# 32 instead of 40 early expert tiles, cut from all but the third row's last 128 tokens, and a new written order for four engines

## The chip, the cores and the metric

One core of a Trainium2 chip runs the whole program. The metric is the device time of one execution in microseconds (us); the kernel before took 429.48 us as the median of three runs (428.34, 429.48 and 429.67). The engines are called PE (matmul), DVE (vector), ACT (scalar), POOL (GpSimd) and SP (the queue that issues most loads). Each engine works through its instructions in order; an instruction that waits holds all behind it.

## The reference

A batch of 4 rows of 512 tokens of 256 features passes a gated linear recurrence with complex state and then a mixture of experts with 32 experts, of which each token takes 6.

```python
x = x + attn(layernorm(x))        # xh = x@W_in; gates; h[t] = a[t]*h[t-1] + xc[t]; h@W_out
xf = layernorm(x).reshape(-1, 256)            # 2048 tokens
scores = sigmoid(xf @ gate_w.T)               # 32 experts in 8 groups
# the 4 groups with the largest maxima stay; the 6 best experts of these are taken
w = chosen_scores / sum(chosen_scores) * 2.5
g, u = xf @ w11[e].T, xf @ w33[e].T           # per expert, 128 wide
y = sum_e  w[t, e] * (silu(g) * u) @ w22[e].T
shared = (silu(xf @ sw1.T) * (xf @ sw3.T)) @ sw2.T
x = x + y + shared
```

All of it is fp32.

## The kernel before

**First part, row by row.** For each row b of 512 tokens the kernel makes the gates (g), the angles (a), the rotated inputs (f) and the scans of the recurrence (s), then the output matmuls with the layer norm and the scores (t), the routing (r) and the shared expert (h). Work of row b+1 is woven into the work of row b. In the lists below a letter with a number names such a piece: r2 is the routing of row 2 (the third row), t3 the attention output of row 3.

**Routing.** `route` (line 522) finds each token's six experts on DVE. Its last products are the weights and `pos` (line 575), the rows of a table `xg` in device memory where the token is to stand, ordered by expert. POOL then issues 24 scatters a row, 4 groups of 128 tokens by 6 choices (`xg<-row,pos`, line 579), 128 rows of 320 numbers each. In rows 0 and 1 a small memset follows each scatter (line 589). A running sum of tokens by expert, `count` (lines 592 and 593), goes from row to row.

**Second part, tiles of 128 tokens of one expert.** The kernel has 112 usual tiles, worked as 56 pairs. `read` (l, line 822) loads a pair's rows from `xg` on the SP queue, four pairs ahead, into four buffers. `spread` (x) transposes them on PE (line 839), ACT copies them (841), DVE picks weights and places (844 to 851). `weights` (k) copies the two experts' up-weights on DVE (859). `up` (u) is 8 matmuls of the pair (871), a silu on ACT (873) and a product on DVE (875). `down` (d) is the second matmul (885), a scaling on ACT (889) into one of six buffers (b_u, b_p, b_th, b_kk, b_s, b_c, by pair number modulo 6), and two scatters on POOL into `zz` (891). At the end the six parts of each token are read back from `zz` (977), added, transposed and written out.

**Early and late tiles.** Which expert a tile belongs to depends on the counts. `tables` (line 651, the pieces ne and nl) makes a table of tiles out of `count`. The early one is made after row 2's routing, from full groups of 128 tokens alone, and its first EARLY tiles may be read before row 3 is routed: their reads wait only for the scatters listed up to then (`puts[:first]`). All other tiles come from the late table and their reads wait for every scatter into `xg`.

**What sets the order.** For PE, DVE, ACT, POOL and SP the kernel holds a written list, `ORDERS`, in which an item such as `r3:24` takes the next 24 instructions of piece r3. `in_order` chains each engine's instructions in that order up to the end of the usual tiles. POOL's lists count two instructions for one scatter (three in rows 0 and 1), PE's list counts matmuls. Every fourth d and k and l item of PE, DVE and SP also loads a few registers.

Of the kernel before, what the change touches and what calls it, by code (L numbers as in the profile page):

```python
# [19 lines left out]
P = 128  # L20
# [29 lines left out]
EARLY = 40  # L50
assert EARLY <= (TOPK * (B - 1) * T - E * (P - 1) + P - 1) // P
# [8 lines left out]
        "g0:24 g1:4 t0 g1:2 t0:4 g1 t0:2 g1 t0 g1:16 g2:8 t0:23 t1 t0 t1:4 h0:2 t1 t0:8 h0 r0 g2 h0 g2:3 t1 g2:4 t1 "  # L60
        "r0:5 g2:8 h0:4 g3:4 t1:3 g3 t1:4 g3:3 t1:9 h0:8 t1:8 h1:3 t2 t1:8 t2:5 r1 h1 g3:4 r1 g3:8 r1:4 t2:2 g3:4 h1:2 "
        "t2:16 h1:9 t2 h1 t2:12 h2:4 t2:3 t3 h2:4 r2:4 t3:2 r2:2 h2:3 t3:4 ne h2:5 t3:7 ne t3:5 d0 ne t3:13 h3:3 t3:3 "
        "h3 t3:5 h3:4 r3:6 h3:5 nl h3 x0:4 h3:2 x1:4 u0:8 x2:4 u1:8 d0 x3:4 d0 u2:8 d1 x4:4 u3:8 d1 d2:2 u4:2 x5:4 u4:6 "
        "d3:2 x6 u5 x6:3 u5 d4 nl u5:6 d4 u6:5 d4 u6:3 nl x7:4 x8:4 d5:2 d6 u7:8 x9 d6 x9:3 x10:4 u8:8 u9:2 x11:2 u9:2 "
        "x11 u9:4 x11 d7:2 x12 u10:2 x12:2 u10:3 x12 u10:3 x13 d8:3 d9 u11:5 d9 u11 x13:2 u11:2 x13 u12 d10:2 u12:5 "
        "x14:3 u12:2 x14 d11 u13:3 x15 u13 d11 u13:2 d12 u13:2 u14:3 d12 x15:3 d12 u14:3 x16:2 u14:2 x16:2 x17:2 u15:2 "
        "d13 x17:2 u15:6 u16 d13 d14 x18 u16:5 d14 x18:3 u16:2 u17:2 x19 d15:2 d16 u17:2 x19:3 u17:4 u18:8 x20:2 d16 "
        "x20:2 d16 d17:2 u19 x21 u19 x21:3 u19:6 d18 u20 x22:3 u20:7 x22 x23 d18 d19 x23 u21:5 d19 x23 d20 x23 u21:3 "
        "u22:2 d20:2 u22:6 u23 x24:4 u23 d21:2 u23:6 d22 x25:4 d22 x26:2 u24 x26:2 u24:7 d23:2 u25:7 d24 u25 x27:4 x28 "
        "u26:3 x28:3 u26:5 u27:2 d24:2 d25 x29:2 d25 x29:2 u27:2 x30:2 u27:4 u28 d26 u28:3 d26 x30 u28:4 x30 d27:2 "  # L70
        "u29:2 d28 u29:2 x31 u29:4 x31:3 x32:3 u30:2 x32 x33 d28:2 u30:6 u31 x33 d29 x33:2 d29 u31:6 x34 u31 u32:6 "
        "x34:2 d30:2 u32:2 x34 x35:4 d31 u33 d31 u33:7 d32:2 u34:4 x36 u34 x36 u34:3 d32 x36:2 u35:2 d33 u35:2 x37 "
        "u35:4 x37 d33 x37:2 u36:3 d34 u36 d34 x38 d35:2 u36:4 u37 x38:2 d36 x38 x39 u37 x39:2 u37 x39 u37:5 d36:2 "
        "u38:2 x40:2 u38:6 x40:2 u39:3 d37 u39 x41:2 d37 u39:3 x41:2 u39 u40:3 d38 x42 d38 u40:5 d39 u41:2 x42:3 d39 "
        "u41:3 x43 u41:3 d40:3 x43:3 x44:3 u42 x44 u42:7 u43:2 d41 u43:4 x45 d41 u43:2 u44:2 x45:2 u44:2 x45 x46 u44:2 "
        "d42:2 u44:2 x46:3 x47 u45:2 x47 u45:3 d43 x47 d43 u45 d44 x47 u45 x48 u45 u46 d44:2 u46:6 x48 u46 x48:2 x49 "
        "d45 u47 x49 u47 x49 u47:5 x49 u47 d45 u48:2 x50:4 u48:6 d46:2 d47:2 d48 u49:4 x51 u49:4 d48 x51:3 d48 x52 u50 "
        "x52 u50:7 x52:2 d49:2 x53:3 u51:5 x53 u51:3 d50:2 u52:3 x54 u52:5 x54:3 x55:2 d51:2 x55 u53:8 x55 d52:3 u54:8 "
        "d53:2 u55:8 d54:2 d55:2",
    ET.DVE:  # L80
        "c cc:3 c:5 cc:11 c:3 cc:3 g0 cc g0:2 c g0:2 c g0:17 cc g1 a0 g1 cc a0:2 g1 a0:2 c a0 g1 a0:2 f0 g1 a0 g1:5 a0 "
        "g1:4 a0 g1:8 a0:2 f0 a0:2 f0 a0:2 f0:2 s0 a0:3 s0:8 a1 g2 a1 g2:2 a1 g2:2 a1 g2 a1:4 t0 g2 t0:2 a1:2 t0:2 g2 "
        "t0:17 f1 a1 f1:2 a1:5 f1 a1 f1 s1 r0:26 a1 r0 a1:2 r0 s1 r0:6 s1:3 h0 r0 s1:3 a2 s1 a2:3 r0 a2:4 f2 h0 g3 a2 "
        "t1 g3:5 t1:2 g3 t1:2 g3 t1:17 a2 f2 a2:5 f2 a2:2 f2:2 s2 a2:2 r1 a2 r1 s2 r1:4 s2:2 r1:28 s2:5 a3:8 h1 t2 a3:2 "
        "t2:2 a3 t2:10 h1 t2:9 f3 a3 f3 a3:4 f3:2 r1 a3 r1 f3 s3 a3:3 h2 s3:2 r2:23 s3 r2 h2 r2:12 s3:2 ne s3:3 ne:15 "
        "t3 ne t3:2 k0 x0 t3:3 ne t3:16 h3 r3 k0 r3:21 h3 r3:2 k0 k1 r3:12 k1 x0:3 nl x1:3 u0 nl:2 k2 nl k2 k3 x1 k3 u1 "
        "x2:3 k4 nl:2 k4:2 u2 x2 x3:2 nl:2 x3:2 x4:3 k5:2 x4 nl u3 k6:2 nl:6 x5 nl:3 x5 u4 x5:2 x6:2 nl:3 u5 q0 k7:2 x6 "
        "u6 x6 x7 k8 x7 nl:2 k8:2 k9:2 nl x7:2 x8:4 x9:2 u7 q1 k10:2 u8 k11 x9 k11 k12 x9 x10:4 x11:2 k12:2 u9 u10 q2 "
        "x11 k13 x11 k13 x12:4 k14 u11 x13:2 u12 k14 x13:2 x14 k15:2 k16:3 u13 x14:3 x15:2 u14 x15:2 x16:2 k17:2 k18:2 "
        "x16:2 x17:2 u15 u16 x17:2 x18:3 u17 k19:2 k20 x18 x19:2 k20 u18 x19:2 k20 k21:2 k22:2 x20 u19 x20 k23 x20:2 "  # L90
        "x21:3 k23 u20 x21 x22:2 k24:2 x22:2 u21 x23:2 k24 k25:2 u22 k26 x23:2 x24:4 u23 k26 k27 x25:4 k27 x26:2 u24 "
        "x26:2 q3 u25 x27 k28:2 x27 k28 k29 x27 u26 x27 x28:4 x29:3 u27 k29 u28 k30:2 k31 x29 x30:2 k31 k32 x30:2 u29 "
        "k32 x31:4 u30 x32:2 k32 k33:2 u31 k34:2 x32 u32 x32 k35 x33:4 x34 k35 u33 k36 x34:3 u34 x35:2 k36:2 x35:2 "
        "k37:2 u35 x36:4 k38:2 k39 x37:4 x38:4 u36 x39:2 u37 k39 k40:3 u38 k41:2 x39:2 k42 x40:2 u39 x40:2 x41 k42 x41 "
        "k43:2 x41:2 x42 u40 k44:2 x42:3 x43:2 k44 x43:2 x44 u41 k45 x44:3 x45:2 u42 k45 x45 u43 u44 k46 x45 k46 x46:2 "
        "k47 u45 k47 x46:2 x47 k48 x47 k48 u46 x47:2 x48:2 k48 k49 u47 k49 x48:2 k50:2 x49 k51:2 u48 x49 k52 x49:2 "
        "x50:2 u49 x50:2 x51:2 k52:2 x51:2 x52:2 k53 u50 x52:2 x53:4 u51 k53 x54 k54:2 k55 x54 k55 u52 u53 x54 u54 x54 "
        "x55:4 u55",
    ET.Activation:
        "cc b0:2 g0:9 a0:2 g0:3 a0:8 g1:2 a0 g1:2 a0 g1:2 a0:2 b1:2 g1:4 a1:2 g1:2 a1:8 t0:4 p0:2 a1 t0:2 a1:2 t0 g2:4 "  # L100
        "a1 g2:4 h0 g2 a2:2 g2:3 h0 a2:3 b2:2 a2:4 h0:2 t1:4 a2:2 t1:2 a2 p1:2 a2:2 t1 g3:8 h1 g3 b3 a3:2 g3:3 a3:2 h1 "
        "a3:2 b3 a3:5 t2:4 h1:2 t2:2 a3:3 h2 p2 t2 p2 h2:3 t3:2 p3 t3:2 p3 t3:2 h3 t3 h3:2 x0 x1 u0 x2 h3 u1 x3 u2 d0:2 "
        "x4 u3 d1:2 x5 u4 d2:2 x6 u5 d3:2 d4:2 u6 x7 x8 u7 x9 d5 u8 x10 d5 d6:2 u9 x11 d7 u10 d7 d8:2 x12 d9 x13 u11 d9 "
        "d10:2 u12 x14 d11 u13 x15 d11 d12:2 u14 x16 u15 x17 x18 u16 d13:2 d14:2 u17 d15:2 x19 x20 d16 u18 d16 d17:2 "
        "u19 x21 u20 d18:2 x22 u21 x23 d19:2 u22 d20:2 x24 d21 u23 d21 d22 x25 d22 x26 u24 u25 x27 x28 d23:2 u26 d24:2 "
        "d25:2 u27 x29 x30 u28 d26:2 d27:2 x31 u29 d28 x32 u30 d28 u31 x33 d29:2 u32 d30 x34 d30 x35 u33 u34 x36 d31:2 "
        "d32:2 u35 d33:2 x37 d34:2 d35:2 u36 x38 u37 x39 u38 x40 d36:2 d37 u39 x41 d37 u40 d38:2 d39 x42 d39 u41 x43 "
        "d40:2 u42 x44 d41:2 u43 x45 d42:2 u44 x46 d43:2 u45 x47 u46 x48 d44:2 u47 d45:2 x49 x50 u48 d46:2 d47:2 u49 "
        "x51 d48:2 x52 u50 d49 u51 d49 x53 d50:2 u52 x54 d51:2 u53 x55 d52:2 u54 d53:2 u55 d54:2 d55:2",
    ET.Pool:  # L110
        "c:10 r0:72 r1:71 r2:48 r3:24 d0:4 d1:2 r3:4 d1:2 d2:4 r3:2 d3:4 d4:4 d5:4 d6:2 r3:8 d6:2 r3:10 d7:4 d8:4 d9:4 "
        "d10:4 d11:4 d12:4 d13:4 d14:4 d15:2 r1 d15:2 d16:4 d17:4 d18:4 d19:4 d20:4 d21:4 d22:4 d23:4 d24:4 d25:4 d26:4 "
        "d27:4 d28:4 d29:4 d30:4 d31:4 d32:4 d33:4 d34:4 d35:4 d36:4 d37:4 d38:4 d39:4 d40:4 d41:4 d42:4 d43:4 d44:4 "
        "d45:4 d46:4 d47:4 d48:4 d49:4 d50:4 d51:4 d52:4 d53:4 d54:4 d55:4",
    ET.SP:
        "c i0 c:7 i1 c:3 w:10 i2 c:3 w c w:54 p0 i3 h0 p1 h1 wl:2 p2 wl h2 l0 wl:5 p3 l0:2 l1:2 l2:2 l3:2 l4:3 l5:2 h3 "
        "l6:2 l7 o0 l7 l8 o0 l8:2 o1 l9:2 l10:2 o1 l11:2 l12:3 l13:2 o2:2 l14:2 o3 l15:2 l16 o3 l16:2 l17:2 l18:2 l19:2 "
        "l20:3 l21:2 l22:2 l23:2 l24:3 l25:2 l26:2 l27:2 l28:3 l29:2 l30:2 l31:2 l32:3 l33:2 l34:2 l35:2 l36:3 l37:2 "
        "l38:2 l39:2 l40:3 l41:2 l42:2 l43:2 l44:3 l45:2 l46:2 l47:2 l48:3 l49:2 l50:2 l51:2 l52:3 l53:2 l54:2 l55:2",
}  # L120


@with_exitstack
def kernel(ctx, tc, x, w_in, w_gx, w_ga, vecs, w_out, gate, w11, w33, w22, sw1, sw3, sw2, out):

# [378 lines left out]

    idle = const.tile([1, 256], mybir.dt.bfloat16, name="idle")
    count = const.tile([P, E], F32, name="count")  # L510
    V.memset(count, 0.0)

    def scores(b, xn2):
        pl = (ps_m if b < B - 1 else ps_x).tile([P, NT, E], F32, tag="m" if b < B - 1 else "x1", name=f"pl_{b}")
# [543 lines left out]
```

## Time and profile before

| what | value |
|---|---|
| median of three runs | 429.48 us |
| the profiled execution, whole | 428.31 us |
| its span, first to last instruction | 426.4 us |
| mean granted clock of PE | 0.916 |
| PE busy | 346.3 us, 81% of the span |
| DVE busy | 303.1 us, 71% |
| ACT busy | 231.8 us, 54% |
| POOL busy | 236.4 us, 55% |
| scatters into xg, 96 | 105.6 us, mean 1.10 |
| scatters into zz, 112 | 115.0 us, mean 1.03 |

The profiled execution took 428.31 us, of which the span is 426.4 us; the other 1.9 us lie before the first and after the last instruction. A timeline row gives the start and the duration in us, the engine, the line, the operation with what it writes and reads, the number of instructions, and in brackets the idle time of the engine before it with what ended that time. Lines are those of the kernel before.

### The profile page before, as it was taken

The numbers are of one execution on the slowest core, as the hardware profiler recorded it, in microseconds if no ns is written. First come the engines' busy times: TensorE is split into PE (matmuls) and PEld (weight loads), VectorE is DVE, ScalarE is ACT, GpSimd is POOL, SyncE is SP. The second block draws the span as 40 slices with busy tenths as digits, with TensorE's granted clock in tenths as the row PEclk, the third lists the DMA queues.
The fourth block names the chain that finished last, engine by engine and source line by source line (L and its number), as shares of the span: only waits on it lengthen the run. The fifth ranks groups of instructions, "written<-read, shape, count | busy, mean of one in ns | idle before, by whom it ended". The sixth has DMA issues, their size and how long they took to land.

```text
span 426.4 us, 7569 instructions
## 1 busy us (share of the span) xinstructions
PE 346.3 (81%) x2074; PEld 281.8 (66%) x2074; DVE 303.1 (71%) x995; ACT 231.8 (54%) x435; POOL 236.4 (55%) x269
## 2 busy tenths in 40 slices
PE   1754787897999888499999999999999999930376
PEld 1332266455646546356999999999999999920276
DVE  5169989999999999517588755776586567412884
ACT  2399957698978871151455545655464555520023
POOL 1000000088879998775777777777777777750000
PEclk9995986999799899978999999999999999995569
DMA  5999871124422375684999966665565655227996
GB/s 154 367 279 302 244 214 49 50 78 157 158 86 100 137 255 206 226 323 154 332 317 358 361 222 203 223 211 170 161 203 177 198 184 190 92 70 309 419 412 240
DMA packets 63868, 91.58 MB, mean 215 GB/s; under 512 B 8517, under 2 KB 53069, under 8 KB 63824
## 3 DMA queue, kind: packets, MB, share of 16 engines
q1 hardware_dynamic: 52000, 56.18, 41.8%
q0 software_dynamic: 9984, 28.33, 17.8%
q10 hardware_dynamic: 1840, 6.55, 3.8%
q8 instruction: 18, 0.29, 0.3%
q14 instruction: 26, 0.21, 0.2%
HBM read 51.19 MB, written 41.94 MB: 218 GB/s over the span
## 4 chain that ended last, share of the span: by engine, by line
PE 42%; DMA 9%; POOL 2%; issue 1%; SPq 0%; ACT 0%; ACTq 0%; POOLq 0%
PE gu L871 22%; PE y L885 11%; PE pxt L839 6%; DMA w_all<-zz 5%; DMA zz<-b_u,place 2%; PE pz L1001 2%; PE pz L1002 2%; POOL zz L891 1%; DMA b_x<-xg 1%; POOL xg L579 1%; DMA xg<-row,pos 1%; SPq L822 0%; ACT o L1004 0%; ACTq L977 0%; PE pbl L711 0%
## 5 line engine op out<-in xcount | busy, mean ns | idle before, releaser
L579 POOL DMA_INDIRECT xg<-row,pos x96 | 105.6, 1100 | 110.0 <-ACT xh L395 83.1
L885 PE MATMUL y<-w_all,b_ga 128*128 x224 | 60.8, 381 | 0.1
L875 DVE TENSOR_TENSOR b_ga<-b_gx,gu 128x256 f32<-128x256 f32 x56 | 23.4, 417 | 37.2 <-ACT b_gx L873 33.2
L873 ACT ACTIVATE b_gx<-gu 128x256 f32<-128x256 f32 x56 | 21.6, 386 | 40.7 <-PE gu L871 36.3
L885 PEld LDWEIGHTS y<-w_all,b_ga 128*128 128x128 f32 x224 | 36.7, 191 | 2.8 <-DVE b_ga L875 0.7
L1001 PE MATMUL pz<-ident,w_all 128*128 128x128 f32 x64 | 14.9, 321 | 27.6 <-DVE w_all L997 17.3
L1001 PEld LDWEIGHTS pz<-ident,w_all 128*128 128x128 f32 x64 | 11.8, 230 | 28.3 <-issue 17.7
L1004 ACT COPY o<-pz 128x256 f32<-128x256 f32 x16 | 5.9, 373 | 39.8 <-DVE w_all L987 30.1
L987 DVE TENSOR_TENSOR w_all<-w_all 128x768 f32<-128x768 f32 x14 | 13.2, 957 | 18.9 <-DMA w_all<-zz 18.9
L891 POOL DMA_INDIRECT zz<-b_u,place x20 | 21.9, 1095 | 6.2 <-issue 1.8
L891 POOL DMA_INDIRECT zz<-b_p,place x20 | 20.2, 1010 | 6.1 <-issue 1.8
L841 ACT COPY b_sphi<-pxt 128x512 f32<-128x512 f32 x28 | 16.4, 585 | 12.0 <-PE gu L871 6.2
L891 POOL DMA_INDIRECT zz<-b_c,place x18 | 18.6, 1032 | 5.6 <-issue 2.1
L849 DVE TENSOR_REDUCE cd<-pick 128x4 f32<-128x128 f32 x56 | 15.8, 281 | 8.3 <-ACT b_c L889 3.1
L841 ACT COPY b_cphi<-pxt 128x512 f32<-128x512 f32 x28 | 16.3, 584 | 9.6 <-PE pxt L839 7.9
L891 POOL DMA_INDIRECT zz<-b_s,place x18 | 18.3, 1017 | 5.5 <-issue 1.8
L891 POOL DMA_INDIRECT zz<-b_th,place x18 | 18.2, 1009 | 5.5 <-issue 2.4
L891 POOL DMA_INDIRECT zz<-b_kk,place x18 | 17.8, 989 | 5.3 <-issue 1.5
L358 PE MATMUL pt<-ident,row 128*128 128x128 f32 x32 | 9.7, 404 | 12.9 <-ACT row L350 7.0
L394 PE MATMUL ph<-xn,win_sb 128*128 128x512 f32 x32 | 18.3, 723 | 1.1 <-ACT xn L359 1.1
L358 PE MATMUL pt<-ident,xnt 128*128 128x128 f32 x32 | 7.4, 358 | 14.2 <-ACT xnt L350 14.2
L647 PE MATMUL sy<-s,sa 128*128 128x256 f32 x64 | 17.3, 416 | 1.1 <-DVE sa L640 1.1
(350 smaller groups left out, 1065.5 us busy)
## 6 DMA issues: line engine op xcount, KB each, us to landing
w_all<-in_w_dram SPq DMA_DIRECT2D x64, 128.0 KB
w_all<-zz SPq DMA_DIRECT2D x7, 768.0 KB
w_all<-zz ACTq DMA_DIRECT2D x7, 768.0 KB
xg<-blank SPq DMA_DIRECT2D x1, 5120.0 KB
b_xh<-xg SPq DMA_DIRECT2D x28, 160.0 KB
b_x<-xg SPq DMA_DIRECT2D x28, 160.0 KB
b_xn<-xg SPq DMA_DIRECT2D x28, 160.0 KB
b_xnt<-xg SPq DMA_DIRECT2D x28, 160.0 KB
```

Source lines behind the costliest of these rows:

```text
L358: PE.transpose(pt[:, j * P : (j + 1) * P], src[j][:, k * P : (k + 1) * P], ident)
L394: PE.matmul(ph, win_sb[:, k, m * P : (m + 1) * P], xn[:, k], start=(k == 0), stop=(k == KC - 1))
L579: i = GP.indirect_dma_start(out=xg[:, :], out_offset=bass.IndirectOffsetOnAxis(ap=pos[:, t, k : k + 1], axis=0), in_=row[:, t], in_offset= ...
L647: PE.matmul(py[:, i], a[:, k, j * P : (j + 1) * P], s2[:, k], start=(k == 0), stop=(k == NSH - 1))
L839: PE.transpose(pt[:, i, k], rows[:, i, k * P : (k + 1) * P], ident)
L841: A.copy(xt, pt)
L871: PE.matmul(gu[:, w, i], w1[:, k, w], xt[:, i, k], start=(k == 0), stop=(k == KC - 1))
L873: A.activation(s, gu[:, 0], AF.Silu)
L875: V.tensor_tensor(a, s, gu[:, 1], ALU.mult)
L885: m = PE.matmul(py[:, i], a[:, i], w2[:, bass.ds(e, 1)].rearrange("p o d -> p (o d)"), start=True, stop=True)
L891: s = GP.indirect_dma_start(out=zz.rearrange("t k d -> (t k) d"), out_offset=bass.IndirectOffsetOnAxis(ap=place[:, i : i + 1], axis=0), in ...
L1001: PE.matmul(pt[:, k], z[:, 0, cut], ident, start=True, stop=False)
```

## The change

EARLY falls from 40 to 32. The early table is now made from a new sum `sure`, which leaves out the last 128 tokens of row 2: two more DVE instructions add it up. The last six scatters of row 2 no longer hold the early reads, so these wait for 66 scatters instead of 72. The lists of PE, DVE, ACT and POOL are new; in SP's list only `h3` and the items `o0`, `o1` (reads of the tokens' own part) move by a few places.

```diff
-EARLY = 40
-assert EARLY <= (TOPK * (B - 1) * T - E * (P - 1) + P - 1) // P
+EARLY = 32
+assert EARLY <= (TOPK * ((B - 1) * T - P) - E * (P - 1) + P - 1) // P
...
     ET.PE:
...
-        "t2:16 h1:9 t2 h1 t2:12 h2:4 t2:3 t3 h2:4 r2:4 t3:2 r2:2 h2:3 t3:4 ne h2:5 t3:7 ne t3:5 d0 ne t3:13 h3:3 t3:3 "
-        "h3 t3:5 h3:4 r3:6 h3:5 nl h3 x0:4 h3:2 x1:4 u0:8 x2:4 u1:8 d0 x3:4 d0 u2:8 d1 x4:4 u3:8 d1 d2:2 u4:2 x5:4 u4:6 "
...
+        "h2:2 t2:4 h2:4 t2:4 r2 h2:2 r2 t3:3 h2 t3:2 h2 r2:4 h2 t3:2 h2:5 t3 ne t3:10 ne t3:5 d0 ne t3:9 h3 t3 h3:2 "
+        "t3:7 h3 r3 h3:4 r3:5 h3 x0:4 h3:5 x1:4 nl h3:2 u0:8 x2:4 u1:8 d0:2 x3:2 u2 x3:2 u2:7 u3:2 x4:4 u3:2 d1 u3 d1 "
...
     ET.DVE:
...
-        "t0:17 f1 a1 f1:2 a1:5 f1 a1 f1 s1 r0:26 a1 r0 a1:2 r0 s1 r0:6 s1:3 h0 r0 s1:3 a2 s1 a2:3 r0 a2:4 f2 h0 g3 a2 "
-        "t1 g3:5 t1:2 g3 t1:2 g3 t1:17 a2 f2 a2:5 f2 a2:2 f2:2 s2 a2:2 r1 a2 r1 s2 r1:4 s2:2 r1:28 s2:5 a3:8 h1 t2 a3:2 "
-        "t2:2 a3 t2:10 h1 t2:9 f3 a3 f3 a3:4 f3:2 r1 a3 r1 f3 s3 a3:3 h2 s3:2 r2:23 s3 r2 h2 r2:12 s3:2 ne s3:3 ne:15 "
-        "t3 ne t3:2 k0 x0 t3:3 ne t3:16 h3 r3 k0 r3:21 h3 r3:2 k0 k1 r3:12 k1 x0:3 nl x1:3 u0 nl:2 k2 nl k2 k3 x1 k3 u1 "
...
+        "a1 f1 a1:5 f1:2 a1:2 f1 s1 r0:14 a1 r0:2 a1:2 r0:2 s1 r0:9 s1 r0:6 h0 r0 s1:4 a2 s1:2 a2 g3 a2:2 g3 a2 g3 a2:2 "
+        "h0 a2 t1 f2 t1:2 r0 g3 t1 a2 g3 t1 g3:2 t1:2 g3 t1:15 a2:3 f2:2 a2:5 f2:2 s2 a2 r0 a2 r1 a2 r1:9 s2 r1:2 s2 "
+        "r1:4 s2 r1:11 s2 r1:7 s2 r1 s2:3 a3:5 t2:3 a3:3 h1 a3 t2:14 h1 t2:5 f3 a3:3 f3 a3 f3 a3:3 f3 a3 f3 h2 s3 a3:3 "
+        "r2 s3 r2:4 s3 r2:5 r1 r2 s3 r2:7 h2 r2:7 s3 r2:10 s3 r2 s3:3 r2 ne:14 t3:3 ne:3 t3:5 r2 t3 k0 t3:4 x0 t3:9 "
+        "r3:6 h3 r3:21 h3 r3:9 ne x0:3 k0:2 x1:4 x2 k1:2 k2:2 k3:2 u0 x2:2 nl:2 k4 x2 nl x3:3 u1 nl:2 x3 x4:3 k4:2 nl "
...
     ET.Activation:
...
-        "a1 g2:4 h0 g2 a2:2 g2:3 h0 a2:3 b2:2 a2:4 h0:2 t1:4 a2:2 t1:2 a2 p1:2 a2:2 t1 g3:8 h1 g3 b3 a3:2 g3:3 a3:2 h1 "
...
-        "x4 u3 d1:2 x5 u4 d2:2 x6 u5 d3:2 d4:2 u6 x7 x8 u7 x9 d5 u8 x10 d5 d6:2 u9 x11 d7 u10 d7 d8:2 x12 d9 x13 u11 d9 "
...
+        "u1 d0:2 x3 u2 x4 d1 u3 x5 d1 u4 d2:2 d3:2 x6 u5 d4:2 x7 x8 u6 d5:2 u7 x9 u8 x10 d6:2 d7:2 x11 u9 u10 x12 d8:2 "
+        "u11 x13 x14 u12 d9:2 d10:2 u13 x15 x16 u14 d11:2 d12:2 x17 u15 u16 d13:2 d14 x18 d14 u17 x19 d15:2 u18 d16:2 "
...
     ET.Pool:
-        "c:10 r0:72 r1:71 r2:48 r3:24 d0:4 d1:2 r3:4 d1:2 d2:4 r3:2 d3:4 d4:4 d5:4 d6:2 r3:8 d6:2 r3:10 d7:4 d8:4 d9:4 "
...
+        "c:10 r0:72 r1:71 r2:48 r3:14 d0:2 r3:6 d0:2 r3:6 d1:4 d2:4 r3:22 d3:4 d4:4 d5:4 d6:4 d7:4 d8:4 d9:4 d10:4 "
...
@@ route
-                if b == B - 1:
+                if b == B - 1 or (b, t) == (B - 2, NT - 1):
                     tc.add_to_no_dep_group("last", i.ins)
...
         more = sm("more", E)
+        if b == B - 2:
+            V.tensor_reduce(more, sel[:, : NT - 1].rearrange("p t e -> p e t"), AX.X, ALU.add)
+            V.tensor_tensor(sure, count, more, ALU.add)
...
@@ after the rows
-    first = len(puts)
-    early, taken = tables(True, None)
+    first = len(puts) - TOPK
+    early, taken = tables(True, None, sure)
...
-    late, _ = tables(False, taken)
+    late, _ = tables(False, taken, count)
```

How the lists move single instructions, engine by engine, is told in the prediction where a step needs it.

## The prediction

> **What bounds the kernel now.** I read the busy slices first, then POOL's timeline, then the timelines of DVE, SP, PE and ACT at the places that POOL's gaps point to, and last the end of the chain of waits.
>
> ```profile
> PE   1754787897999888499999999999999999930376
> DVE  5169989999999999517588755776586567412884
> POOL 1000000088879998775777777777777777750000
> ```
>
> A slice is 10.66 us. PE is full from slice 18 to 33, and DVE from slice 3 to 14. POOL shows only 7 in the pair phase, but a scatter is 0.97 busy and the next starts 0.30 later at the soonest, so 7 is POOL working back to back.
>
> ```profile
> 126.08 1.14 POOL L579 DMA_INDIRECT xg<-row,pos  x1 [2.03 <-issue]
> ...
> 164.49 1.00 POOL L579 DMA_INDIRECT xg<-row,pos  x1 [0.17 <-issue]
> 165.79 0.98 POOL L579 DMA_INDIRECT xg<-row,pos  x1 [0.30 <-issue]
> ...
> 188.04 0.97 POOL L579 DMA_INDIRECT xg<-row,pos  x1 [0.30 <-issue]
> ...
> 195.73 1.09 POOL L579 DMA_INDIRECT xg<-row,pos  x1 [0.30 <-issue]
> 199.58 0.97 POOL L579 DMA_INDIRECT xg<-row,pos  x1 [2.76 <-issue]
> ...
> 376.46 0.97 POOL L891 DMA_INDIRECT zz<-b_u,place  x1 [0.40 <-ACT b_u L889]
> ...
> 380.29 0.97 POOL L891 DMA_INDIRECT zz<-b_p,place  x1 [0.30 <-DMA zz<-b_u,place]
> ```
>
> These are the first and last scatter of row 1, the first, 18th and last of row 2, the first of row 3 and two of the last. Between 126 and 380 POOL stands only once for more than its step: 2.76 before row 3. From there 136 scatters run without a hole, (380.29 - 199.58) / 135 = 1.339 each. Gaps of 0.40 near the end, released by ACT's scaling, say that PE and ACT are just in time there. After the last scatter the read-back starts at 385.01 and the rest ends at 426.4: a fixed tail of 46.1 after the last scatter's start. So the end is: start of row 3's scatters, plus 135 steps, plus the tail.
>
> ```profile
> 125.12 0.18 DVE L575 TENSOR_SCALAR pos<-top 128x32 int32<-128x32 f32 x1
> 125.21 2.33 DVE L501 TENSOR_TENSOR_SCAN g<-ga,y 128x512 f32<-128x512 f32 x2
> ...
> 198.63 0.18 DVE L575 TENSOR_SCALAR pos<-top 128x32 int32<-128x32 f32 x1
> ```
>
> pos of row 1 ends at 125.30 and POOL starts 0.78 later; in row 3 it is 198.81 and 0.77. In rows 1 and 3 pos is what POOL waits for. In row 2 pos stood ready at 163.07, 2.7 before its first scatter, so row 2 follows row 1 without a hole.
>
> **The change, part by part.** I walk each queue in the new order with the durations of before.
>
> Row 0's pos. L452 (0.68) stood at 60.16, in the shadow of DVE's wait that ended at 61.95; it now comes after L482, inside the full stretch: about +0.6. ACT puts four normalisations L350 (1.93 together) ahead of the sigmoid's table load, which makes `grp` 1.1 later (about 77.3 for 76.19). On DVE L497 (0.68) and L640 (0.66) move ahead of L575. Of this 3.0, some 0.7 overlaps the wait for ACT: pos ends about 87.0 instead of 84.61. Row 0's scatters then end near 126.1 instead of 123.8. That binds nothing unless row 1's pos is as early as before.
>
> Row 1's pos. One scan L501 (pitch 1.15) now runs ahead of L575 instead of behind it; of the earlier lateness 0.55 to 1.1 is left, the rest being work that has moved behind pos. So pos ends 1.7 to 2.25 later; I take 1.7, since DVE's work ahead of it, added up, is the surer count. Row 1's scatters start at 127.8, with a gap before them as now.
>
> Row 2. POOL goes on without a hole, so +1.7: its last scatter is at 197.4 and POOL is free for the next at 197.4 + 1.09 + 0.30 = 198.8. Row 2's pos has 2.7 of slack and takes the moved scan (1.15); the two added DVE instructions for `sure` (like L592 and L593, 0.36 + 0.19) go behind it, where DVE has holes (9.97 before L640 at 189.84), so I cost them at nothing.
>
> Row 3's pos. What it removes: two passes of the shared expert ahead of the scores, 0.87 as they run at 188.63 to 190.60 and up to 1.7 as at 183.76; three weight copies L859 (0.43, 0.40, 0.42, of which two stand right in the route at 195.97). What it adds: one L640 (0.68). That makes pos end near 197.6 instead of 198.81, and POOL could take it at 198.4. POOL itself is free at 198.8 (above), so this is late by 0.4 no more: row 3 starts at 198.8 instead of 199.58, **-0.8**. The hole of 2.76 closes to 0.30 (-2.46) and 1.7 of that is eaten by row 1.
>
> A page rule bears on the two passes, and nothing below rests on it. In the rows L638 takes 0.90 a pass at 183.76 and 0.49 after 188, PE having come out of a thin stretch. The Trainium skill, "TensorE: Matmul & The Clock Gate", Part 1, says the slow warm-up is a budget of about 3.4 us of time, not a number of matmuls. By that rule dropping two passes does not drop slow ones, and saves 0.87, not 1.7; the sum is the same by either, as POOL's own end decides.
>
> The early read. It waits for 66 scatters, so for the 18th of row 2: 188.04 + 1.7 = 189.7 instead of 195.73.
>
> ```profile
> 198.54 0.90 SPq L822 DMA_DIRECT2D b_xh<-xg  x2
> ```
>
> The read was issued 2.8 after the last scatter's start, so now at 192.5, 6 us sooner, and the rows are there at 195.4 (2.87 after issue, as at 201.41 now). But PE is then at row 3's routing and the first output passes; the first transpose comes near 196.8 (201.5 now) and the first pair's up matmul at 200.9:
>
> ```profile
> 203.69 0.50 PE L871 MATMUL gu<-b_sphi,b_wph 128*128 128x128 f32 x3
> ```
>
> So PE gains 2.8 on POOL's 0.8 and begins the pairs with more lead.
>
> The later reads. Pair 16 (l16) was early and is now late: it waits for row 3's last scatter. That one moves from POOL slot 38 to slot 30, so to 198.8 + 29 x 1.339 = 237.6, landed 240.2. Before, l16 was issued at 240.08. Nothing is lost. SP's moved items (one load for the shared expert, two reads of the tokens' own part) pass reads of 0.33 to 0.9 us in a queue that waits for slots anyway; POOL's one leftover instruction of row 1 moves from d15 to d12. Both at nothing; if SP's order held a pair's read back, its lead of four pairs (4 x 3.10) is the cover.
>
> The ring of six buffers. Row 3's scatters end sooner, so d3 moves to slots 31 and 32 and d4 and on behind it, and d9's scaling waits for d3's second scatter: 240.3 + 3.4 (as the b_p row below follows 252.57) = 243.7.
>
> ```profile
> 256.01 0.84 ACT L889 ACTIVATE b_p<-y,cd 128x256 f32<-128x256 f32 x2
> ...
> 246.07 0.60 PE L885 MATMUL y<-w_all,b_ga 128*128 x2
> ```
>
> PE's new order has u14, x15 and x16 to run meanwhile; d12's y needs the space that d10's scaling frees (243.7 + four scalings of 0.85 pitch with what lies between: 247.2), and PE gets there about 245.2: it stands about 2.0. At 246.07 before, PE was at the same pair d12; it then has done 2.1 more of other work (five y of 0.22, nine up passes of 0.11). So of its 2.8 lead about 1.0 is left (247.2 - 246.07 against 2.1), and 0.8 is what POOL's earlier start needs. Bounds: -2.8 if PE never stands, +2.6 if it stands one more round of two scatters.
>
> The sum for the profiled execution: 428.31 - 0.8 = 427.5. Its time is 1.17 under the median of 429.48; the same -0.8 on the median gives **428.7**. The steps' bounds: row 1 later by 1.7 to 2.25 adds 0.55; row 1 not late at all takes 1.7 off, till the whole 2.46 is won.
>
> **The rivals.**
> A, the forecast: -0.8, 428.7. For it: the two gaps in the rows and POOL's hole-free run.
> B, row 1 is not late (DVE's holes elsewhere swallow the moved scan, or the row 0 lateness does not reach it), and pos 3 comes sooner still: -2.46, 427.0. Against it: no DVE hole over 0.15 between 63 and 171.
> C, PE and not POOL sets the end: 56 pairs of 3.10 (16 x 0.11 + 4 x 0.22 + transposes) is 173.2, which is just the time from 203.69 to the last y near 376.9; then the whole -2.8 counts, 426.7. For it: the 0.40 gaps released by ACT. Against it: only five of 135 gaps are longer than 0.31.
> D, **slower**: the ring of six. In ACT's new order d9's and d10's scalings stand ahead of u13 and x15, so while ACT waits at 243.7 for d3's landing, silu and copies behind it wait too, DVE's product after them, and PE with that. It decides as soon as PE reaches d12's equivalent later than 246.07 by more than the 0.3 that POOL's gaps allow. Price: one round of two scatters, 2.6, so 429.48 + 2.6 = 432.1. For it: in before PE lost nothing at d13 although d7's scaling waited to 256.01, because PE was behind; a PE that leads meets the wait.
> E, row 1 is late by 3.0 (the pr matmuls of row 0 now queue behind 3.6 us of L394): POOL then ends row 2 at 200.1 and row 3 starts 0.5 later than now, 430.0. For it: POOL has no slack between row 1 and row 2.
>
> **How the numbers follow.** About 0.3% (1.3 us) is what a measurement of this kernel can tell from no change: 428.19 to 430.77 counts as the same. A has 0.38, B 0.20, C 0.14, D 0.19, E 0.09. A lies 0.5 above the lower bound with an own spread of some 1.2, so a third of it is faster (0.13), the rest the same; B and C are faster but for a tenth (0.31); D is slower (0.18), E splits (0.06 the same, 0.03 slower), and of A 0.02 is slower. Faster 0.43, same 0.34, slower 0.23. The likeliest's own range is 427.5 to 429.9; with B, C and D's nearer part 426.0 to 431.8.
>
> **What would show it.** Row 1's first scatter at 127.8, later than 126.08; row 3's at 198.8 with a gap near 0.30 before it; the first early read issued near 192.5; the first up matmul near 200.9; PE standing some 2 us about 245; the steps of 1.339 unbroken. It is wrong if row 1 starts no later (B), if the last scatters wait for ACT by more than 0.3 each (C or D, by their start), or if the mean step after row 3's start differs from 1.339 by 0.01, which alone is 1.35 us.

## The result and the profile after

The changed kernel takes 425.92 us (median of 20 runs, 424.61 to 430.32) against 428.79 for the kernel before in runs beside it (20 runs, 426.88 to 431.87): a ratio of 0.994 with an interval of 0.9922 to 0.9958, about 2.6 us (the two medians differ by 2.87). It is faster, by three times what was forecast. Its profiled execution has a span of 423.7 us against 426.4.

First the same three rows of busy slices, then POOL's timeline of the kernel after: the first scatter of row 1, the first, 18th and last of row 2, the first of row 3, and the late ones.

```profile
PE   1735859996999889399989999999999999930376
DVE  6089989999999998357777376567477656412884
POOL 1000000098898998777777777777776767750000
```

```profile
125.09 1.01 POOL L580 DMA_INDIRECT xg<-row,pos  x1 [0.17 <-issue]
...
164.13 0.97 POOL L580 DMA_INDIRECT xg<-row,pos  x1 [0.31 <-issue]
...
195.03 1.07 POOL L580 DMA_INDIRECT xg<-row,pos  x1 [0.30 <-issue]
...
327.31 0.97 POOL L896 DMA_INDIRECT zz<-b_p,place  x1 [2.12 <-ACT b_p L894]
...
350.07 1.03 POOL L896 DMA_INDIRECT zz<-b_kk,place  x1 [2.18 <-ACT b_kk L894]
...
377.83 0.97 POOL L896 DMA_INDIRECT zz<-b_p,place  x1 [0.31 <-issue]
```

Both holes of before, 2.03 ahead of row 1 and 2.76 ahead of row 3, are closed; row 3 starts at 195.03 instead of 199.58, 4.55 earlier. But the last scatter comes only 2.46 earlier (377.83 for 380.29). Between them stand two new holes of 2.12 and 2.18, released by ACT's scaling of PE's results: POOL waits for PE. PE's row has an 8 in its 21st slice, in the pair phase, where before it was full. The next three are rows of SP's, PE's and ACT's timelines of the kernel after:

```profile
188.48 0.90 SPq L827 DMA_DIRECT2D b_xh<-xg  x2
```

```profile
196.24 1.05 PE L876 MATMUL gu<-b_sphi,b_wph 128*128 128x128 f32 x8
...
215.31 1.10 PE L890 MATMUL y<-w_all,b_ga 128*128 x4 [1.63 <-DVE b_ga L880]
...
243.97 0.44 PE L844 MATMUL pxt<-ident,b_x 128*128 128x128 f32 x2 [1.31 <-DMA b_x<-xg]
244.49 1.99 PE L890 MATMUL y<-w_all,b_ga 128*128 x8
```

```profile
243.97 0.47 ACT L894 ACTIVATE b_s<-y,cd 128x256 f32<-128x256 f32 x1 [1.61 <-DMA zz<-b_s,place]
```

PE's pairs start 7.45 earlier than before (196.24 for 203.69), and PE then stands 3.84 in the pair phase: 1.63 behind DVE, 1.31 at 244, which is put down to the rows of pair 17, the second of the late ones, and 0.90 (at 261) behind the ring of six buffers. Before it stood for nothing there. The ACT row is the ring itself: the scaling of pair 10 waits until pair 4's scatter has landed, which is at the moment when pair 17's rows come.

In the table, "u" is the first up matmul of pair 0, "y" the start of the last down matmul, and the last column the start of the last scatter; "stands" adds PE's gaps over 0.12 in the pair phase. All are times of one profiled execution, in us. Those of e1, e2 and e4 lie -2.0, +1.8 and +2.2 from the medians of their kernels, so that landmarks of two rows compare only to about that.

| kernel | row 3's first scatter | u | PE stands | y | last scatter |
|---|---|---|---|---|---|
| before | 199.58 | 203.69 | 0 | 376.49 | 380.29 |
| after | 195.03 | 196.24 | 3.84 | 374.03 | 377.83 |
| e1_head60 | 196.24 | 200.49 | 0.17 | 373.59 | 377.39 |
| e2_head165 | 197.28 | 206.44 | 0.94 | 380.79 | 384.60 |
| e3_cut32 | 198.56 | 200.94 | 8.66 | 385.45 | 389.26 |
| e4_tail60 | 196.84 | 197.52 | 2.89 | 376.94 | 380.74 |
| e9_all72 | 194.88 | 196.10 | 2.17 | 373.63 | 377.43 |
| e10_pace1 | 191.96 | 194.27 | 3.38 | 371.58 | 375.39 |
| e11_late16 | 196.01 | 197.43 | 3.12 | 374.58 | 378.38 |
| e12_read72 | 197.26 | 208.55 | 1.45 | 383.19 | 387.00 |

Two regularities are in it. The last scatter starts 3.80 or 3.81 after the last y in every row: PE's last pair ends the phase, whatever POOL did. And y is u plus 172.8 (what before took without a gap) plus what PE stands, plus 0.1 to 1.2; where the granted clock fell after a stand (e3, e4, e9), 2.6 to 3.7 are lost besides.

### The profile page after: what moved, and what is told of

Same layout as the page of the kernel before. It is cut to its first block, busy times and chain, and to the rows that moved or that the text cites. A ratio compares the mean times of both kernels' runs of the same rounds, so it can differ in the third digit from the quotient of the medians.

```text
span 423.7 us, 7579 instructions
## 1 busy us (share of the span) xinstructions
PE 344.4 (81%) x2074; PEld 280.5 (66%) x2074; DVE 300.6 (71%) x997; ACT 231.2 (55%) x435; POOL 235.1 (55%) x269
## 4 chain that ended last, share of the span: by engine, by line
PE 42%; DVE 22%; DMA 13%; POOL 8%; issue 7%; ACT 6%; POOLq 0%; SPq 0%; DVEq 0%; ACTq 0%
PE gu L876 20%; PE y L890 9%; POOL xg L580 6%; DMA w_all<-zz 5%; PE pxt L844 5%; DMA zz<-b_s,place 2%; DMA zz<-b_u,place 2%; PE pz L1006 2%; PE pz L1007 2%; DVE st L336 1%; DMA xg<-row,pos 1%; ACT row L350 1%; DMA b_xnt<-xg 1%; DVE w_all L501 1%; DMA x<-in_x_dram 1%
## 5 line engine op out<-in xcount | busy, mean ns | idle before, releaser
L580 POOL DMA_INDIRECT xg<-row,pos x96 | 107.6, 1121 | 104.7 <-DVE pos L576 82.3
L896 POOL DMA_INDIRECT zz<-b_u,place x20 | 20.4, 1021 | 6.4 <-issue 2.1
L358 PE MATMUL pt<-ident,row 128*128 128x128 f32 x32 | 7.9, 362 | 14.7 <-ACT row L350 7.7
L358 PEld LDWEIGHTS pt<-ident,row 128*128 128x128 f32 x32 | 4.7, 171 | 18.0 <-ACT row L350 10.6
```

The source lines that it names most:

```text
L358: PE.transpose(pt[:, j * P : (j + 1) * P], src[j][:, k * P : (k + 1) * P], ident)
L580: i = GP.indirect_dma_start(out=xg[:, :], out_offset=bass.IndirectOffsetOnAxis(ap=pos[:, t, k : k + 1], axis=0), in_=row[:, t], in_offset= ...
L896: s = GP.indirect_dma_start(out=zz.rearrange("t k d -> (t k) d"), out_offset=bass.IndirectOffsetOnAxis(ap=place[:, i : i + 1], axis=0), in ...
```

## The experiments

The first four split the change: by time (the new order up to some point, the old one after it, or the reverse), and the cut without the lists. A list is split by giving each engine the new list's items that had started by that time, then the old list's items that are left.

**e1_head60.** New order of PE, DVE and ACT in the first 60 us only.

```diff
 ET.PE:
-  "g0:24 g1:4 t0 g1:2 t0:4 g1 t0:2 g1 t0 g1:16 g2:8 t0:23 t1 t0 t1:4 ..."
+  "g0:23 g1:4 g0 t0:6 g1:2 t0:2 g1:18 g2:8 t0:23 t1 t0 t1:4 ..."
```

> The kernel before, with the new order of PE, DVE and ACT only for what these engines start in the first 60 us; from there on the old order, and the early cut stays at 40. Theory S (the first 60 us give the gain: row 0's statistics end at 59.90 instead of 62.51, and the lead is handed on through all rows): pos of row 0 near 82, row 1's first scatter near 123.6 instead of 126.08, row 3's first near 197.1 instead of 199.58, the whole 2 to 2.5 us faster (ratio 0.994 to 0.995). Rival R (the lead is lost again on the way, and the gain is made after row 2's routing): row 3's first scatter within 0.7 of 199.58, ratio 0.998 to 1.002.

Measured: ratio 1.0002 (0.997 to 1.0033). No gain that can be told. The profiled execution has the landmarks of theory S (row 1's first scatter at 123.60, row 3's at 196.24), but it is 2.0 under the median, and over all runs the time does not move; the interval leaves out theory S's 0.994 to 0.995. What the first 60 us give is hidden in their own scatter: the last statistics instruction of row 0 starts at 62.51, 61.14 and 61.74 in three profiles with the old first stretch, and between 59.55 and 62.08 in eleven with the new one (mean 60.5). Theory S falls as a theory of the gain.

**e2_head165.** New order through row 2's routing, old order and old cut after it.

```diff
 ET.DVE:
-  "... r2:23 s3 r2 h2 r2:12 s3:2 ne s3:3 ne:15 ..."
+  "... r2:4 s3 r2:5 r1 r2 s3 r2:7 h2 r2:7 s3 r2:10 s3 ..."
```

> As the run before, but with the new order up to 164.5 us (through row 2's routing), then the old order with the cut at 40 and the early reads waiting for all 72 scatters. Theory S: row 1's first scatter near 125.1, row 2's last near 193.6, pos of row 3 35.7 after that of row 2 as in the old order, near 195.4, row 3's first scatter near 196.2, first up matmul near 201.5; 2 to 3.4 us faster (ratio 0.992 to 0.995). Rival R: pos of row 3 stays at 198 to 199 because row 3's stretch of the list is what was shortened; ratio 0.998 to 1.001.

Measured: ratio 1.0047 (1.0012 to 1.0081), slower, which neither theory had. Row 3's first scatter came 2.30 earlier than before, and the end 4.31 later. This contradicts the prediction's sum outright: row 3's start on POOL went one way and the end the other. PE's timeline of this run has the reason:

```profile
202.20 0.69 PE L842 MATMUL pxt<-ident,b_xh 128*128 128x128 f32 x2 [4.65 <-DMA b_xh<-xg]
...
206.44 0.85 PE L874 MATMUL gu<-b_sphi,b_wph 128*128 128x128 f32 x3
```

PE is ready for pair 0 and stands 4.65 for its rows, which wait for row 2's last scatter (195.98); u is 2.75 later than before, PE then stands 0.94, and the end follows u. POOL in its turn stands 2.70 at pair 0's scatter (215.19), waiting for ACT and so for PE.

**e3_cut32.** The cut alone: 32 early tiles, the new sum, reads after 66 scatters, all with the old lists.

```diff
-EARLY = 40
+EARLY = 32
...
-    first = len(puts)
+    first = len(puts) - TOPK
...
 ET.DVE:
-  "... h2 r2:12 s3:2 ne ..."
+  "... h2 r2:14 s3:2 ne ..."
```

> The changed code (32 early tiles, the sum without the last 128 tokens, early reads after 66 scatters) with the old order of all engines; the two added DVE instructions stand at the end of row 2's routing. Theory S: the early read is issued near 190.7 but PE's old order puts ten output passes ahead of the first transpose, so the first up matmul comes at most 1.2 sooner than 203.69; pair 16 now waits for row 3's last scatter, which the old POOL list has at slot 38 (near 250), so its rows come near 256 instead of 243 and PE stands 4 to 8 us: 3 to 7 us slower than before (ratio 1.007 to 1.016). Rival C (the cut alone gives the gain): ratio 0.993 to 0.997.

Measured: ratio 1.0197 (1.0159 to 1.0235), some 9 us slower; more than the 3 to 7 expected. u did come 2.75 earlier. But pair 16 is now a late one, and the old POOL list has row 3's last scatter at slot 38 (247.98), so SP issues its read at 250.79. PE's windows of this run (stretch, length, PE's busy time and instructions, granted clock, DMA share, GB/s), and the row that ends the wait:

```profile
236.00:246.00 10.00, 9.35 (x73) 1.00 0.73 269
246.00:256.00 10.00, 1.99 (x9) 0.68 0.58 180
256.00:266.00 10.00, 10.00 (x62) 0.81 0.68 229
```

```profile
253.25 0.66 PE L846 MATMUL pxt<-ident,b_xh 128*128 128x128 f32 x2 [7.90 <-DMA b_xh<-xg]
```

PE stands 7.90, and comes back at a lower granted clock: 62 instructions in the next 10 us where a full stretch has about 80. That is 3.1 us more, and most of the surplus over what was expected.

**e4_tail60.** The whole change, but the old order in the first 62 us.

```diff
 ET.PE:
-  "g0:23 g1:4 g0 t0:6 g1:2 t0:2 g1:18 g2:8 t0:24 t1:3 h0:2 t0:8 ..."
+  "g0:24 g1:4 t0 g1:2 t0:4 g1 t0:2 g1 t0 g1:16 g2:8 t0:24 t1:3 h0:2 t0:8 ..."
```

> The changed code with the old order in the first 62 us and the new order after that: what is left of the change without its first stretch. Theory S: the lead of 2.5 us is gone, all after it is the new order, so pos of row 0 near 86.1, row 1's first scatter near 127.5, row 3's first near 197.3, first up matmul near 198.8, and the whole within 1 us of before (ratio 0.997 to 1.002). The prediction on record, which left the first 60 us as they were, said row 1's first scatter 127.8 and row 3's 198.8, -0.8 us. Rival R (the later part of the list gives the gain): ratio 0.994 to 0.996, as the whole change.

Measured: ratio 0.9952 (0.9928 to 0.9975), against 0.994 for the whole change: rival R, the gain is made after the first 62 us. With e1 the two agree.

The next four went to a chip on which the kernel before itself took 496.91 us. In e5 PE stops for 8.49 at 187, for nothing that the trace names. Within that group the four can be compared with before, but not with each other (their intervals are half a per cent either way, and all overlap).

**e5_all72** (the edit is `first = len(puts)`), **e6_orders40** (the kernel before with all new lists, `EARLY = 40`, less two DVE items), **e7_pace1** and **e8_late16** (edits below).

> The changed kernel, but the early reads wait for all 72 scatters of rows 0 to 2 again; the 32 early tiles, the sum and every list stay. Two chains may set the end: PE's (start of the first up matmul, 56 pairs without a hole 172.8, plus what PE stands) and POOL's (row 3's first scatter, the slots up to the pair whose buffer is waited for, then PE's rest). Theory P (PE's chain decides): first early read near 196.4 instead of 188.5, first up matmul near 203 instead of 196.24, some of the 3.84 that PE stands vanishes, last y 2 to 5 us later; 2 to 5 us slower than the changed kernel, ratio to before 0.999 to 1.006. Theory Q (POOL's row 3 start decides, as the prediction had it): row 3's first scatter stays near 195.0 and so does the end; ratio 0.992 to 0.996.

> The kernel before (40 early tiles, no extra sum, early reads after 72 scatters) with all the new lists, less the two DVE instructions that it has not. Theory P: first up matmul as late as in the run before this (near 203), but pair 16 is early again and is not waited for, so it is 0 to 1.5 us faster than that one: ratio 0.996 to 1.004. If the lists alone were the gain and the cut did nothing: ratio 0.992 to 0.996.

> The changed kernel without the small memset behind each scatter of row 1, so that row 1's scatters follow each other at 1.28 to 1.4 instead of 1.45 to 1.55. Both chains: row 2's first scatter near 160.7 (its pos is done at 159.8) instead of 164.1, row 3's near 192 instead of 195.0 (its pos at 191.2), row 3's last near 231.9, pair 16's read and the ring's landings 3 us sooner, so PE's standing of 1.31 and 0.90 goes and the end comes 1.5 to 3 us sooner than in the changed kernel: ratio to before 0.987 to 0.991. If only PE's start counts: 196.24 stays, ratio 0.992 to 0.996. If unpaced scatters slow the loads and copies of row 2 down: pos of row 2 and 3 come over 1 us later, ratio over 0.996.

> The changed kernel with the order round pair 16 loosened: PE runs pair 15's eight up matmuls before the transposes of pair 16, ACT takes pair 13's silu before the two scalings of pair 9 that wait for buffers, pair 14's before pair 10's, and DVE's two products move along. If PE's standing at 244 (1.31, and 2.9 with a slower clock after it in the run with the old first stretch) is a matter of order: it vanishes, 0.5 to 2 us faster than the changed kernel, ratio to before 0.989 to 0.993. If the ring of six buffers (POOL's slots) holds the pairs anyway: the time is only moved to the next waits, ratio 0.993 to 0.996.

Measured: 0.9876 (0.9821 to 0.9931), 0.9885 (0.9828 to 0.9942), 0.9881 (0.9824 to 0.9937) and 0.9883 (0.9846 to 0.992). On such a chip PE, not the rows' arrival, is late everywhere (u near 209 in e5, e7 and e8, 211 in e6), so no theory is told apart. e5 is in fact the changed kernel (see e9), so that on this chip the lists alone (e6) do as well as the whole change, within the intervals. That does not carry over, and e6 was not run on another chip: what the new lists give with 40 early tiles stays open there. e12 answers the nearest question, with 32.

**e9_all72.** The repeat of e5.

> The same kernel as the first with early reads after all 72 scatters, since that group ran where the kernel before took 497 us and PE stood 8 us at 187 for nothing the trace names. Theory P (PE's chain from the first up matmul): first early read near 196.4, first up matmul near 203, 2 to 5 us slower than the changed kernel, ratio to before 0.999 to 1.006. Theory Q (row 3's start on POOL decides): row 3's first scatter near 195.0 and the end as in the changed kernel, ratio 0.992 to 0.996.

Measured: 0.9927 (0.9901 to 0.9952); first read at 188.50. The edit had no effect: the last six scatters of row 2 were still in the group of which the reads are declared free, so the added wait fell away. What it gives is a second profile of the changed kernel, which agrees with the first to 0.15 us up to u (pos of row 3 at 191.02 and 191.03, u at 196.10 and 196.24), and its time.

**e12_read72.** The same with the group mended, so that the early reads wait for all 72 scatters; all else as in the changed kernel.

```diff
-                if b == B - 1 or (b, t) == (B - 2, NT - 1):
+                if b == B - 1:
...
-    first = len(puts) - TOPK
+    first = len(puts)
```

> The changed kernel with the early reads really behind all 72 scatters of rows 0 to 2 (in the earlier try the last six of row 2 were still in the group that the reads may pass, and the first read was issued at 188.50 as in the changed kernel). All lists, the 32 early tiles and the sum stay. Theory P (PE's chain holds too): first read near 196.4, first up matmul near 202 to 204 instead of 196.24, POOL stands some 6 us before pair 0's first scatter, which its list has at slot 7; 2 to 6 us slower than the changed kernel, ratio to before 0.997 to 1.008. Theory Q (row 3's start on POOL, near 195.0 in both, decides alone, and the cut buys nothing): ratio 0.990 to 0.996.

Measured: ratio 1.0113 (1.0067 to 1.0159). Against the changed kernel's 0.994 that is 1.7%, some 7 us, for one wait. Theory P, with more than its 2 to 6. From this run's SP, PE and POOL timelines:

```profile
198.68 0.90 SPq L827 DMA_DIRECT2D b_xh<-xg  x2
```

```profile
200.97 0.69 PE L844 MATMUL pxt<-ident,b_xh 128*128 128x128 f32 x2 [7.70 <-DMA b_xh<-xg]
...
208.55 1.05 PE L876 MATMUL gu<-b_sphi,b_wph 128*128 128x128 f32 x8
```

```profile
214.37 0.97 POOL L896 DMA_INDIRECT zz<-b_u,place  x1 [8.31 <-ACT b_u L894]
```

PE stands 7.70 with work behind it that doesn't need the rows: the new list has the first transposes ahead of the ten passes of the shared expert that the old one ran first. Then POOL stands 8.31 at pair 0's scatter, although row 3's scatters behind it in the list are ready. So this run delays PE first and POOL through it. (The first stretch was 2.2 later in this execution than in e9, which goes into row 3's start, 197.26; the stand of 7.70 is not from that.)

**e10_pace1.** The changed kernel without the memset behind each scatter of row 1.

```diff
-                if b < B - 2:
+                if b < 1:
                     paced = GP.memset(idle, 0.0)
...
-        "c:10 r0:72 r1:71 r2:48 ... d12:4 r1 d13:4 ..."
+        "c:10 r0:72 r1:48 r2:48 ... d12:4 d13:4 ..."
```

> Again the changed kernel without the memsets behind row 1's scatters. Row 2's first scatter near 161, row 3's near 192 instead of 195.0, last of row 3 near 232. If POOL's chain (row 3's start, the late reads, the ring) holds the pairs: 1.5 to 3 us faster than the changed kernel, ratio to before 0.987 to 0.991. If PE's start alone counts: 0.992 to 0.996. If unpaced scatters slow row 2's and 3's work: over 0.996.

Measured: 424.34 us, ratio 0.9914 (0.9881 to 0.9947); beside it e9, which is the changed kernel, had 425.34 and 0.9927. The intervals overlap, so that it beats the change is not shown by the times. The profile shows the mechanism, in POOL's rows for row 2's and row 3's first scatter and PE's gaps:

```profile
160.81 1.30 POOL L580 DMA_INDIRECT xg<-row,pos  x1 [0.47 <-ACT so L652]
...
191.96 0.97 POOL L580 DMA_INDIRECT xg<-row,pos  x1 [0.40 <-issue]
```

```profile
240.53 0.44 PE L844 MATMUL pxt<-ident,b_x 128*128 128x128 f32 x2 [1.17 <-DMA b_x<-xg]
241.84 1.99 PE L890 MATMUL y<-w_all,b_ga 128*128 x8 [0.86 <-ACT b_s L894]
```

Everything moved by about the same amount: row 3's first scatter 2.9 sooner than in e9, u 1.8, the stand for pair 17's rows from 242.29 to 240.53, the end 2.0. The stand did not go, since PE came sooner as well. Rows 2 and 3 now start 0.77 after their pos is ready, while in e9 pos lies ready for some 4 us before POOL comes to it.

**e11_late16.** The changed kernel with a looser order round pair 16.

```diff
 ET.PE:
-  "... u14:3 x15 x16:4 x17:2 d12:2 d13:2 x17:2 u15:8 x18:2 u16:6 d14 ..."
+  "... u14:3 x15 u15:8 x16:4 d12:2 x17:2 d13:2 x17:2 x18:2 u16:6 d14 ..."
 ET.Activation:
-  "... u12 d9:2 d10:2 u13 x15 x16 u14 d11:2 d12:2 x17 u15 ..."
+  "... u12 u13 d9:2 x15 u14 d10:2 d11:2 x16 u15 d12:2 x17 ..."
```

> Again the changed kernel with the looser order round pair 16 (PE: pair 15's up matmuls before pair 16's transposes; ACT: the silus of pairs 13 and 14 before the scalings of pairs 9 and 10). If the standing at 244 is a matter of order it vanishes: ratio to before 0.989 to 0.993. If POOL's slots hold the pairs anyway, the wait only moves: 0.993 to 0.996.

Measured: 0.9941 (0.991 to 0.9972), no gain. The wait for the late rows has gone, and others stand in its place:

```profile
243.91 1.13 PE L876 MATMUL gu<-b_cphi,b_wph 128*128 128x128 f32 x8 [1.48 <-ACT b_s L894]
249.58 0.44 PE L844 MATMUL pxt<-ident,b_xn 128*128 128x128 f32 x2 [1.05 <-ACT b_sphi L846]
```

Both are released by ACT, which in turn waits for the landing of the scatters of pairs 3, 4 and 5 (1.20, 0.62 and 3.14 in ACT's rows at 241.98, 244.52 and 248.58). So at pairs 9 to 11 it is POOL's slots, through the ring, that hold PE; an order that avoids the wait for the rows meets this one.

## Why the prediction was right, and where it was not

**The sign and the range.** The sign was right and the size was not: -0.8 was forecast, about -2.6 measured. On the prediction's own scale 0.994 of 429.48 is 426.9, which lies in its wide range (426.0 to 431.8) and outside the likeliest's own (427.5 to 429.9). All three signs that it had named for being wrong are there: row 1 starts no later (125.09 for 126.08), late scatters wait for ACT (2.12 and 2.18), and the mean step is 1.354. So the sign is in part luck: the -0.8 stood on a chain that does not set the end by itself. The nearness of rival C's 426.7 is luck too: C had PE start 2.8 earlier and lose nothing, and PE started 7.45 earlier and lost 5.0 of it.

**Row 0's and row 1's pos.** This is the first term that was mis-sized. To take out the first stretch's scatter, each pos is counted from the start of row 0's last statistics instruction, or from the pos before (profiles of the chip with 497 us are left out):

| stretch | old order, 3 profiles | new order, 6 or 7 profiles | difference of means | on record |
|---|---|---|---|---|
| row 0's statistics to pos 0 | 21.92 to 22.41 | 23.27 to 23.63 | +1.5 | +2.4 |
| pos 0 to pos 1 | 40.68 to 41.35 | 39.03 to 39.16 | -1.8 | -0.7 |
| pos 1 to pos 2 | 37.77 to 37.86 | 37.09 to 37.30 | -0.7 | none worked out |
| pos 2 to pos 3 | 34.79 to 35.74 | 31.14 to 31.96 | -3.7 | -2.9 from pos 1 |

Row 1's pos is -0.3 from there and not +1.7. The rise in row 0 is real and has the parts that were named (in the profiles of before and after L452, L497 and L640 add 1.77 by their pitches, and the stretch grows by 1.69). Between pos 0 and pos 1 the scan L501 adds its 1.10 as said, instructions that went ahead of pos 0 take 0.7 off, but those that stand in this stretch in both lists take 2.02 less as well. Moved instructions were costed; the unmoved ones were taken at their old pitch.

For POOL neither row 1's nor row 3's pos counts in the kernel after. pos of rows 1, 2 and 3 is ready at 122.73, 159.81 and 191.21, which is 2.4, 4.3 and 3.8 before POOL takes it. From row 0's pos on POOL works without a hole, and row 3's start is row 0's start (84.61) plus 72 scatters and their memsets, 110.42; before, with two holes, it was 114.04. That POOL's own end would set row 3's start was forecast rightly; that row 1's pos would set row 1's start, at 127.8, was not.

**Row 3's pos.** The second mis-sized term: -4.4 from pos 1, against -2.9. It is PE that gains by it, as its list has row 3's routing ahead of the pairs. In the two profiles of before and after the stretch from pos 2 is 4.34 shorter: the three weight copies give 0.99 and one scan less 1.12; the two added instructions cost 0.29, which the prediction put at nothing for DVE's holes. The L640 that it added (0.68) is not there: two stand in this stretch in both lists. The other 2.5 are almost all unmoved work again that waits less. One such wait was in the trace of before, on PE, in the midst of row 3's attention output; the row below it is the same instruction after:

```profile
171.05 0.27 PE L704 MATMUL ptte<-ident,tcole 128*2 128x128 f32 x1 [1.06 <-DVE tcole L693]
```

```profile
166.85 0.27 PE L708 MATMUL ptte<-ident,tcole 128*2 128x128 f32 x1
```

It stands among the attention matmuls of row 3; the new list puts it four of them further back, and PE no longer stops there. (DVE's statistics behind these matmuls had waited too, 1.08 in all before, 0.06 after.)

**The sum itself** is the step that failed as a mechanism: "start of row 3's scatters, plus 135 steps, plus the tail". The tail is fixed, but the steps stretch: 1.339 each before, 1.354 after, 1.405 in e12. e2 and e12 start row 3 on POOL 2.3 earlier than before and end 4.3 and 6.7 later. In its place stand two chains that take turns. PE's: u, 172.8 for the pairs, and what PE stands. POOL's: row 3's start and the slots up to d3 to d10, which give back the ring's buffers to pairs 9 to 16, and the rows to pair 16. The prediction had PE's chain as rival C with 0.14, and held against it that few of POOL's gaps were over 0.31. A queue with a backlog hides an upstream chain in just that way, and the backlog can be read from the kernel before: pair 8's first scatter starts 16.6 after the end of its scaling on ACT, pair 24's 10.1, pair 40's 5.4, pair 52's 0.27. POOL was working off row 3's scatters and had caught up with PE before the end. The chain that ended last in the kernel before says the same; from the landing of row 2's last scatter and the read behind it, it runs over PE up to 368, and only then over POOL:

```profile
195.73 2.61 DMA xg<-row,pos
200.14 3.23 DMA b_x<-xg
203.41 0.44 PE pxt L839 x2
...
367.61 0.78 PE gu L871 x7
368.76 1.09 issue
369.85 0.97 POOL zz L891
```

**The early read.** Right in mechanism (66 scatters, 2.6 from the 18th's start to the issue: 185.85 to 188.48), too small in size: u was put 2.8 earlier and came 7.45 earlier, as PE was itself free sooner by row 3's gain. The cut was given no part in the sum. e12 shows that it is worth some 7 us in the new order, and e2 that the new first part without it is slower than before.

**Pairs 16 and 17.** "Nothing is lost" failed as it was reasoned. The reckoning of 240.2 for the landing came out near (SP issued at 239.06), but partly by luck, as row 3 had started 3.8 sooner than reckoned; and it was set beside the old demand of 240.08, while PE, 7 us ahead, asked sooner. PE stands 1.31 for pair 17's rows, read right behind pair 16's; in e9 1.10. Yet these rows are not the wait that ends last there. The chain of the kernel after passes through the ring:

```profile
240.10 3.84 DMA zz<-b_s,place
...
243.97 0.48 ACT b_s L894
244.45 0.04 issue
244.49 1.99 PE y L890 x8
```

The y at 244.49 would have waited for ACT's scaling even with the rows in place, and in e11, where the order keeps PE from waiting for the rows, PE waits 1.48 for the same buffer. With the old POOL list the late rows do decide, and cost 7.90 (e3).

**The ring.** The mechanism of rival D is there: ACT waits 1.16, 0.43, 1.43 and 1.61 for landings between 239 and 244, and silus stand behind these. The price of 2.0 for PE's stand about 245 was of the right order: 1.31 in this profile, 1.10 and 0.91 in e9, 1.17 and 0.86 in e10, and another 0.90 at 261 in this one. It did not cost the lead as a whole, since the lead was 7.45 and not 2.8.

What stays open: the 1.63 behind DVE at 215, which is in one of two profiles of the changed kernel (e9 has none); which unmoved instructions wait less for which reason in each row, since no run took them one by one; whether e10 beats the changed kernel by time; and what the new lists give with 40 early tiles on a chip like the first.

## What to carry to other kernels

A cut that lets data be used earlier and the order of the work around it are one change, not two: here the cut with the old lists costs 2.0%, the new lists and the 32 tiles without the early read cost 1.1%, and both together gain 0.6%. When a queue works back to back, look for the chain that fills its backlog before calling it the bound: a run in which one of them starts later and the other sooner (e2) tells which one the end follows. And cost a reordering by its unmoved instructions too, since who stands next to whom sets their pitch and their waits.

## What was not expected of the hardware

**Neighbours on DVE.** Of 128x512 instructions that take 0.68 or 0.69, the next starts 0.60 or so later (0.59 to 0.62) when it shares nothing with the one before but what both read, and 0.70 to 0.73 later when it reads what that one wrote, or writes over what that one read. From DVE's timeline of before, first L464, L465 and L486, then L474 to L476: L475 writes over the `c` that L474 reads, and L476 reads the `c` of L475.

```profile
38.11 0.68 DVE L464 TENSOR_TENSOR ph<-ph,c 128x512 f32<-128x512 f32 x1
38.71 0.69 DVE L465 SCALAR_TENSOR_TENSOR u<-u,s 128x512 f32<-128x512 f32 x1
39.32 0.69 DVE L486 TENSOR_TENSOR y<-xh,sphi 128x512 f32<-128x512 f32 x1
...
44.51 0.68 DVE L474 TENSOR_TENSOR ph<-ph,c 128x512 f32<-128x512 f32 x1
45.23 0.69 DVE L475 TENSOR_TENSOR c<-w,c 128x512 f32<-128x512 f32 x1
45.96 0.69 DVE L476 SCALAR_TENSOR_TENSOR w<-c,ph 128x512 f32<-128x512 f32 x1
```

That dependence is the cause is argued from such rows, not shown by a run made for it. The Trainium skill, "VectorE: DVE Perf Modes", Rules for kernel authors, advises for chained DVE instructions to keep their number low; here their neighbours count too, by 0.12 each.

**The clock after short stands.** In e4 PE stands 1.09, 0.61 and 0.93 within 4 us, none of them long, and the granted clock falls; so it does in e9 (0.94 and 0.89) after 1.10 and 0.91. In the first profile of the changed kernel one stand of 1.31 leaves it at 1.00, and in e10 1.17 and 0.86, as close together as those of e9, leave it at 1.00 too. PE's windows of e4, of e9, of e10 and of the kernel after:

```profile
236.00:246.00 10.00, 7.36 (x53) 0.91 0.60 196
246.00:256.00 10.00, 9.75 (x53) 0.75 0.62 201
```

```profile
236.00:246.00 10.00, 7.83 (x51) 0.94 0.64 208
246.00:256.00 10.00, 10.00 (x74) 0.89 0.56 177
```

```profile
236.00:246.00 10.00, 7.97 (x59) 1.00 0.70 217
246.00:256.00 10.00, 10.00 (x77) 1.00 0.71 214
```

```profile
236.00:246.00 10.00, 8.60 (x63) 1.00 0.70 239
246.00:256.00 10.00, 10.00 (x83) 1.00 0.62 194
```

So short stands can cost about as much again in the ten us behind them (in e4 53 instructions instead of 83), but need not: stands of the same size go either way in e9 and e10, and what decides between the two is not shown. The Trainium skill, "TensorE: Matmul & The Clock Gate", Part 1, gives idle gaps of over some 3.4 us as what brings the slow clock, and for another kernel short idles that come often enough. The 7.90 of e3 agrees with the first and e4 and e9 with the second, which e10 does not bear out.

**The scatter of the start.** The first 60 us of one and the same order end anywhere in a stretch of 2.5 us, and all that follows is shifted with them. Landmarks of two single profiles are therefore best compared from a common point, as in the table of pos.
